# A graph layer with three-digit products: Gelu's result and the last block's sum left in PSUM, and another start

## The chip, the cores and the metric

The kernel runs on one NeuronCore of a Trainium2 chip. The metric is the device time of one execution in microseconds (us). Before the change three runs gave 237.19, 238.38 and 238.70 us; their median is 238.38.

## The reference

One graph layer over 625 nodes of 512 features, 20625 weighted edges and 4 relations. Cut to what is computed:

```
h   = relu(layernorm(x))
msg = sum over r of (h[src] @ W_rel[r] + b_rel[r]) * where(edge_type == r, edge_weight, 0)
agg = segment_sum(msg, dst) / max(segment_sum(edge_weight, dst), 1)
x1  = layernorm(h + h @ W_self + b_self + agg) * ln1_g + ln1_b
ffn = gelu(x1 @ W_ffn1 + b_ffn1) @ W_ffn2 + b_ffn2
out = x + layernorm(x1 + ffn) * ln2_g + ln2_b
```

W_ffn1 is 512 x 1024 and W_ffn2 is 1024 x 512.

## The kernel before

**Tiles.** The nodes lie in five blocks of 125. The engines are TensorE (PE), VectorE (DVE), ScalarE (ACT), GpSimd (POOL) and SyncE (SP, which issues transfers). PSUM is used as eight banks of 128 x 512 words, handed out by `bank(name)`; `row(name)` hands out a row of SBUF.

**Digits.** Most products are not made in f32. An operand is split in a high part, a part between and a low part (fp32r), and three products (high, between, low) replace one f32 product. For Gelu's result g this takes four steps per pair of f: `high_g` (L1135, ACT) rounds g to its high part, `unit_g` (L1138, ACT) scales that up, `between_g` (L1141, DVE) subtracts g, and `low_g` (L1145, DVE) forms the low part. The two DVE steps read g and one other operand.

**Stages.** (1) x is loaded, normalised and turned (`tp_h`, L285; copies `hT`, L671), and multiplied by the weights of the relations into message rows (`pt`, L769; evicted by L777). The first products wait for loads of x (L176, L190, L191), of `firsts` (L194) and of the weights (L188). Ahead of them PE runs warm-up products on `zeros` (L625). (2) DVE decodes the edge lists (L369 to L516; `fields`, L435, go to PE's `tf`, L536) and makes one-hot rows (L557 to L561), which PE adds up (`bank`, L574) and DVE reduces (`sums_w`, L580). (3) Blocks 0 to 2 get their messages by one-hot sums times message rows (`chunk_sum`, L1011). Blocks 3 and 4 get them by 72 indirect transfers that POOL issues (L904), which DVE adds up (L929; the last of them writes `es`), and which PE adds into `acc` (L949, L950, L952). (4) `add_to` (L955) forms the block's sum from `acc`; `block_stats` (L1051), POOL's square root (L280) and `normed` (L1057) make x1; PE turns it (`tp_x`, L285), ACT copies it (`x1T`, L1065). (5) `up` (L1123) makes the first FFN product for one f of eight, into a bank of its own; `act` (L1127) applies Gelu from that bank into a row `gT` in SBUF; the digits follow, and `down` (L1155) makes the second product `po`. (6) `summed` (L1173, L1175), `mean`, the square root, and `normed` (L1187, ACT), `scaled` (L1190, POOL), `added` (L1193, POOL) make the output; POOL also prepares the late copy of x (L1043) and of x1 (L1068, L1071). The last block's end is made in two half columns on DVE (L1197, L1202). Stage 5 is run for blocks 0 and 1 together, 2 and 3 together (250 columns), and 4 alone (125 columns).

**Order.** Every step is handed to the class `Plan` as an `op` with an engine, an estimated duration, its predecessors, a rank, and the buffers that it takes and gives (`ps` are the PSUM banks, `gT` the pairs of f under way). `Plan.times` (L62) goes through time and lets each engine take the best ready op; the code is then emitted in that order, and each engine runs its own instructions strictly in that order. X_AT, W_AT, WARM and `free` are the planner's guesses of when loads arrive. Waits between engines are then set for each tile: an instruction that writes a bank waits for the readers of that bank that were emitted before it, whichever columns they read.

## Time and profile before

| what | before |
| --- | --- |
| median of three runs | 238.38 us |
| the profiled execution's own time | 237.71 us |
| its span | 235.9 us |
| granted TensorE clock | 0.995 |
| PE busy | 220.9 us (94%), 1017 instructions |
| DVE busy | 211.5 us (90%) |
| ACT, POOL busy | 91.5 us, 153.5 us |
| DMA | 43.48 MB, mean 184 GB/s |

The span reaches from the first to the last instruction of the profile; the execution's own time is 1.8 us longer. Rows of the time line give the start in us, the busy time in us, engine, line, operation, output<-inputs, shape, how many instructions the row holds, and in brackets the idle time just before and what ended it. The table of windows gives for each stretch the busy time of each engine. f32 matmuls have two records each.

### The profile page before, as it was taken

What the parts mean: (1) busy time and instruction counts of PE and PEld (TensorE: products, weight loads), DVE (VectorE), ACT (ScalarE), POOL (GpSimd) and SP (SyncE); (2) the same over time, 40 slices, a digit from 0 to 9 for tenths busy, and PEclk for the clock granted to TensorE, in tenths of its full rate; (3) what the DMA queues carried; (4) which work ended last, traced back from release to release, by engine and by line L of the source; (5) the groups of instructions that cost most, each with busy time, mean ns of one, the idle gap of its engine ahead of it and who ended that gap; (6) DMA issues with size and microseconds to landing.
All of it is one profiled execution on the core that took longest, in us unless ns stands there. A gap on an engine that the chain in (4) does not pass through costs nothing. (4 is left out here: it accounts for less than half of the span.)

```text
span 235.9 us, 3270 instructions
## 1 busy us (share of the span) xinstructions
PE 220.9 (94%) x1017; PEld 149.9 (64%) x1017; DVE 211.5 (90%) x404; ACT 91.5 (39%) x181; POOL 153.5 (65%) x167
## 2 busy tenths in 40 slices
PE   6979999999999998999999999999999996999970
PEld 2434445588888786745645444448988884889960
DVE  6996998999999999999999999999999999964542
ACT  2739366494331210103112643225792244635410
POOL 6587830288881067778778778774777899855050
PEclk9999999999999999999999999999999999999997
DMA  6974799868956376789988776678677701100002
GB/s 196 365 236 148 208 259 272 247 164 175 185 136 134 101 257 169 204 332 378 348 280 283 199 208 186 179 213 276 186 199 204 212 6 46 43 0 23 24 3 91
DMA packets 19193, 43.48 MB, mean 184 GB/s; under 512 B 3274, under 2 KB 4180, under 8 KB 19044
## 3 DMA queue, kind: packets, MB, share of 16 engines
q0 software_dynamic: 8272, 22.91, 36.7%
q1 hardware_dynamic: 10498, 19.98, 25.6%
q10 hardware_dynamic: 402, 0.34, 0.5%
q8 instruction: 9, 0.15, 0.3%
q14 instruction: 12, 0.10, 0.1%
HBM read 33.68 MB, written 6.52 MB: 170 GB/s over the span
## 5 line engine op out<-in xcount | busy, mean ns | idle before, releaser
L904 POOL DMA_INDIRECT ms<-table,row_g x72 | 75.7, 1051 | 33.6 <-DVE sums_w L580 12.4
L1011 PE MATMUL acc<-m,sums_w 126*128 126x512 f32 x120 | 53.8, 595 | 0.0
L929 DVE SCALAR_TENSOR_TENSOR ea<-ms,wgt_g,ea 128x512 f32<-128x512 f32 x59 | 41.5, 747 | 0.0
L1011 PEld LDWEIGHTS acc<-m,sums_w 126*128 126x128 f32 x120 | 22.2, 190 | 23.5 <-issue 22.5
L769 PE MATMUL pt<-w,hT 128*128 128x512 f32 x80 | 36.0, 598 | 1.2 <-ACT hT L671 1.2
L1123 PE MATMUL pu<-x1T,w_sb 128*128 128x250 f32 (+1 forms) x192 | 35.7, 341 | 0.0
L1123 PEld LDWEIGHTS pu<-x1T,w_sb 128*128 128x128 f32 x192 | 31.7, 190 | 3.9 <-issue 0.7
L580 DVE TENSOR_REDUCE sums_w<-bank 126x160 f32<-126x480 f32 x48 | 28.0, 651 | 0.0
L769 PEld LDWEIGHTS pt<-w,hT 128*128 128x128 f32 x80 | 14.6, 190 | 17.0 <-issue 13.9
L910 ACT ACTIVATE ea<-ms,groups 128x512 f32<-128x512 f32 x12 | 8.4, 698 | 37.1 <-DMA ms<-table,row_g 36.8
L777 ACT ACTIVATE m<-pt,rx 125x512 f32<-125x512 f32 x20 | 13.7, 685 | 21.9 <-PE pt L769 19.3
L574 PEld LDWEIGHTS <-w_first 128*128 128x128 bf16 x192 | 14.1, 148 | 7.6 <-issue 4.8
L1155 PE MATMUL po<-w_digits,ghigh 128*125 128x512 f32 (+1 forms) x48 | 17.8, 372 | 0.0
L1141 DVE TENSOR_TENSOR gbetween<-glow,gT 128x500 fp32r<-128x500 f32 (+1 forms) x12 | 12.2, 1018 | 6.0 <-ACT glow L1138 6.0
L515 POOL DMA_INDIRECT groups<-in_edge_groups_dram,first_g x12 | 14.5, 1211 | 4.4 <-issue 2.7
L1155 PE MATMUL po<-w_low,glow 128*125 128x512 f32 (+1 forms) x48 | 17.1, 356 | 0.0
L750 POOL DMA_DIRECT2D wd<-w x8 | 8.0, 1188 | 13.7 <-PE pt L769 10.4
L915 ACT CAST eh<-ea 128x512 fp32r<-128x512 f32 x11 | 6.5, 593 | 26.6 <-DVE ea L929 26.5
L574 PE MATMUL bank<-w_first 128*128 128x120 bf16 x192 | 15.5, 227 | 1.3 <-DVE z L780 0.9
L1127 ACT ACTIVATE gT<-pu,cols 128x250 f32<-128x250 f32 (+1 forms) x24 | 10.5, 439 | 13.4 <-PE pu L1123 13.3
L769 PE MATMUL pt<-w_l,hl 128*128 128x512 f32 x40 | 15.7, 392 | 0.0
L769 PE MATMUL pt<-wd,hd 128*128 128x512 f32 x40 | 15.6, 390 | 0.0
(199 smaller groups left out, 415.9 us busy)
## 6 DMA issues: line engine op xcount, KB each, us to landing
table<-m SPq DMA_DIRECT2D x20, 224.0 KB
w<-in_L_gnn_W_rel_dram SPq DMA_DIRECT2D x16, 256.0 KB
wd<-w POOLq DMA_DIRECT2D x8, 256.0 KB, 6.0
w_sb<-in_L_gnn_W_ffn_dram SPq DMA_DIRECT2D x2, 1024.0 KB
w<-in_L_gnn_W_ffn_dram SPq DMA_DIRECT2D x8, 256.0 KB
x_late<-in_x_dram SPq DMA_DIRECT2D x1, 1280.0 KB
ms<-table,row_g POOLq DMA_INDIRECT x72, 3.7
w<-in_L_gnn_W_self_dram SPq DMA_DIRECT2D x4, 256.0 KB
```

Of the source, the lines that this page charges most:

```text
L515: nc.gpsimd.indirect_dma_start(out=groups[:, k].rearrange("p f q -> p (f q)"), out_offset=None, in_=edge_groups[:, :], in_offset=bass.Indi ...
L574: nc.tensor.matmul(p[:, i * W:(i + 1) * W], low[:, t // TB, :, t % TB], high[:, t // TP, :, t % TP], start=True, stop=True)
L580: nc.vector.tensor_reduce(sums_w[OUTER[d]][:NG + 1, :, n0:n0 + 2 * QT].rearrange("p c (t h) -> p t h c", h=2), p[:NG + 1, :QT * 3 * HB].re ...
L769: nc.tensor.matmul(box["p"], x_[:, k, :], w_, start=(k == 0 and n == 0), stop=(k == KD - 1 and n == len(pairs) - 1))
L777: nc.scalar.activation(kept[c][:NG], box["p"][:NG], AF.Copy, scale=rx[:NG, i, root_of(i, r)])
L904: nc.gpsimd.indirect_dma_start(out=ms[j], out_offset=None, in_=table[:, :], in_offset=bass.IndirectOffsetOnAxis(ap=row_g[:, j // EG, j % E ...
L929: nc.vector.scalar_tensor_tensor(to, ms[j], wgt_g[:, k, q - 1:q], box["sum"], op0=ALU.mult, op1=ALU.add)
L1011: nc.tensor.matmul(acc[b,], sums_w[b][:NG + 1, c, :], kept[c][:NG + 1], start=first, stop=last)
L1123: nc.tensor.matmul(p[:, :self.n], w1_sb[0][:, k, f * P:(f + 1) * P], self.x1T()[:, k, :self.n], start=(k == 0), stop=(k == KD - 1))
L1127: nc.scalar.activation(self.gT[f][:, :self.n], self.pu[f][:, :self.n], AF.Gelu, bias=bf1[:, f:f + 1])
L1141: nc.vector.tensor_sub(self.digits(f, "between"), self.low[f, "pair"].bitcast(F32), self.pair[f][:, :, :self.n])
L1155: nc.tensor.matmul(p[:at.stop - at.start, :c.stop - c.start], g_[:, at], w_[:, c], start=(f == 0 and n == 0), stop=(f == KF - 1 and n == l ...
```

## The change

1. **First loads.** The load of x's second block and of `firsts` are issued by ACT in place of SP, so that the four first weight pieces and the rest of x come two places earlier in SP's queue.
2. **Zeros first.** DVE's clearing of `deg_4` and `brel` moves behind the clearing of `zeros`, as an op of the plan; nine warm-up products in place of ten. The planner's guesses (X_AT, W_AT, `free`) are set anew.
3. **Gelu in PSUM.** `up` takes one bank for two f (blocks in pairs) or four f (last block). `act` writes Gelu's result over its own input in that bank. `high_g`, `between_g` and `low_g` read it there. The bank is given back after the last `low_g` on it; `gT` stands at 8 in place of 6.
4. **Last sum in PSUM.** For block 4, `add_to` writes its result into the `acc` bank, and `block_stats` and `normed` read it there; the bank is given back after `normed`.

The diff, cut to its core:

```
-    nc.sync.dma_start(xs[:, 0, :D // 2], x[:P, :D // 2])
-    load_w(0, 0)
-    load_x(xs, 1, 2)
-    nc.sync.dma_start(first_of_tile, firsts)
-    for k in range(1, KD):
+    nc.sync.dma_start(xs[:, 0, :D // 2], x[:P, :D // 2])
+    load_x(xs, 1, 2, nc.scalar)
+    nc.scalar.dma_start(first_of_tile, firsts)
+    for k in range(KD):
         load_w(0, k)
...
-    nc.vector.memset(deg_4, 0.0)
-    nc.vector.memset(brel, 0.0)
+    def cleared():
+        nc.vector.memset(deg_4, 0.0)
+        nc.vector.memset(brel, 0.0)
...
-    WARM = 10
+    WARM = 9
...
-    X_AT = [3.55, 5.4, 9.0, 10.7, 10.7]
-    W_AT = [4.3, 6.7, 7.4, 8.4]
+    X_AT = [3.2, 5.1, 8.0, 9.7, 9.7]
+    W_AT = [4.6, 5.6, 6.4, 7.2]
...
     def add_to(b, of, rows_):
-        nc.vector.scalar_tensor_tensor(z[rows_, b, :], of()[rows_, :], rdeg[rows_, b:b + 1], z[rows_, b, :],
+        sum_of[b] = of() if b == NB - 1 else z[:, b, :]
+        nc.vector.scalar_tensor_tensor(sum_of[b][rows_, :], of()[rows_, :], rdeg[rows_, b:b + 1], z[rows_, b, :],
...
+            self.per = 2 if n > P else 4
...
         def up(self, f):
-            if f % 2 == 0:
-                t = row(f"gT_{self.name}_{f}", F32, (P, 2, 2 * P))
-                self.gT.update({f: t[:, 0], f + 1: t[:, 1]})
-                self.pair[f] = t
-            p = self.pu[f] = bank(f"pu_{self.name}_{f}")
+            m = self.per
+            if f % m == 0:
+                t = bank(f"pu_{self.name}_{f}", (P, m, D // m))
+                self.pu.update({f + q: t[:, q] for q in range(m)})
+                self.pair.update({f + q: t[:, q:q + 2] for q in range(0, m, 2)})
+                if not self.split:
+                    t = row(f"gT_{self.name}_{f}", F32, (P, m, D // m))
+                self.gT.update({f + q: t[:, q] for q in range(m)})
+            p = self.pu[f]
```

The changed code's line numbers are 2 to 12 higher: `up` is L1135, `act` L1139, `high_g` L1147, `down` L1167.

**Place 1: PE in the last block.** `pu_…` is the bank of an `up`, `po_0_2091` and `po_0_2037` are the second product of block 3 (the number counts its column half); "waits Activation" means a wait for ACT. Before:

```order
L1123 MATMUL pu_0_2055<-x1T_2042,w_sb 128x125 [waits Activation_49] x4
L1123 MATMUL pu_1_2064<-x1T_2042,w_sb 128x125 x4
L1123 MATMUL pu_2_2071<-x1T_2042,w_sb 128x125 x4
L1123 MATMUL pu_3_2081<-x1T_2042,w_sb 128x125 x4
L1155 MATMUL po_0_2091<-w_digits_1458,ghigh_0_1928 125x512
```

With the change:

```order
L1167 MATMUL po_0_2037<-w_low,glow_0_1919 125x512
L1135 MATMUL pu_0_2048<-x1T_2031,w_sb 128x125 [waits Activation_49] x4
L1135 MATMUL pu_0_2048<-x1T_2031,w_sb 128x125 x4
L1135 MATMUL pu_0_2048<-x1T_2031,w_sb 128x125 [waits Activation_49]
L1135 MATMUL pu_0_2048<-x1T_2031,w_sb 128x125 x3
L1135 MATMUL pu_0_2048<-x1T_2031,w_sb 128x125 [waits Activation_49]
L1135 MATMUL pu_0_2048<-x1T_2031,w_sb 128x125 x3
L1135 MATMUL pu_4_2077<-x1T_2031,w_sb 128x125 x12
L1135 MATMUL pu_4_2077<-x1T_2031,w_sb 128x125 [waits Activation_49]
L1135 MATMUL pu_4_2077<-x1T_2031,w_sb 128x125 x3
L1167 MATMUL po_0_2037<-w_digits_1460,ghigh_2_1939 125x512
```

Before, the eight `up` stood in two groups of four with twelve products of block 3 between them. Now six products of block 3 stand ahead, all eight `up` follow in one run, and eighteen products of block 3 stand behind. The third, fourth and eighth `up` carry a wait for ACT (the first four rows' wait, for the turned x1, is there in both).

**Place 2: ACT in the last block.** `y_2060` and `y_2044` are block 2's output rows; the store of them stands on ACT's queue. Before:

```order
L1127 ACTIVATE gT_0_2054<-pu_0_2055,cols 128x125 [waits PE_49]
L1127 ACTIVATE gT_0_2054<-pu_1_2064,cols 128x125 [waits PE_49]
L1135 ACTIVATE ghigh_0_2086<-gT_0_2054 128x2x125 [waits Activation_49]
L1138 ACTIVATE glow_0_2089<-ghigh_0_2086 128x2x125 [waits Activation_49]
L1127 ACTIVATE gT_2_2070<-pu_2_2071,cols 128x125 [waits PE_49]
L1187 ACTIVATE y_2060<-y_2060,mv_y_2076 125x512 [waits DMASW1_49,DVE_49,Pool_49]
L1127 ACTIVATE gT_2_2070<-pu_3_2081,cols 128x125 [waits PE_49]
```

With the change:

```order
L1139 ACTIVATE pu_0_2048<-pu_0_2048,cols 128x125 [waits DVE_49,PE_49]
L1199 ACTIVATE y_2044<-y_2044,mv_y_2053 125x512 [waits DVE_49,Pool_49]
L1139 ACTIVATE pu_0_2048<-pu_0_2048,cols 128x125 [waits PE_49,Activation_49]
L1147 ACTIVATE ghigh_0_2074<-pu_0_2048 128x2x125 [waits PE_49,Activation_49]
L1139 ACTIVATE pu_0_2048<-pu_0_2048,cols 128x125 [waits Activation_49]
L1150 ACTIVATE glow_0_2082<-ghigh_0_2074 128x2x125
L1139 ACTIVATE pu_0_2048<-pu_0_2048,cols 128x125 [waits Activation_49]
L1147 ACTIVATE ghigh_2_2092<-pu_0_2048 128x2x125 [waits DVE_49]
L1150 ACTIVATE glow_2_2095<-ghigh_2_2092 128x2x125 [waits DMASW5_49,DMASW0_49,Activation_49]
L1112 DMA out_dram<-y_2044 13x512 [waits Pool_49]
L1139 ACTIVATE pu_4_2077<-pu_4_2077,cols 128x125 [waits PE_49]
L1139 ACTIVATE pu_4_2077<-pu_4_2077,cols 128x125 [waits Activation_49]
```

Gelu now writes the tile that it reads. The normalisation of block 2 moved ahead of the second Gelu, the first `high_g` waits for PE (the fourth `up`), the second `high_g` for DVE (the first `between_g`), and the fifth and sixth Gelu stand behind the store.

**Place 3: SP at the start.** `xs` is x, `w_…` the weight pieces, `w_first` the table `firsts`. Before:

```order
L191 DMA xs<-in_x_dram 128x256
L188 DMA w_0_77<-in_L_gnn_W_rel_dram 128x512
L176 DMA xs<-in_x_dram 128x512
L194 DMA w_first<-in_firsts_dram 128x162
L188 DMA w_1_81<-in_L_gnn_W_rel_dram 128x512
L188 DMA w_2_83<-in_L_gnn_W_rel_dram 128x512
L188 DMA w_3_85<-in_L_gnn_W_rel_dram 128x512
L176 DMA xs<-in_x_dram 128x512 [waits DMAHW0_49]
L176 DMA xs<-in_x_dram 128x2x512 [waits DMAHW1_49]
```

With the change:

```order
L191 DMA xs<-in_x_dram 128x256
L188 DMA w_0_79<-in_L_gnn_W_rel_dram 128x512
L188 DMA w_1_81<-in_L_gnn_W_rel_dram 128x512
L188 DMA w_2_83<-in_L_gnn_W_rel_dram 128x512
L188 DMA w_3_85<-in_L_gnn_W_rel_dram 128x512
L176 DMA xs<-in_x_dram 128x512 [waits DMAHW0_49]
L176 DMA xs<-in_x_dram 128x2x512 [waits DMAHW1_49]
```

Two issues left SP's queue ahead of the second weight piece; both now stand on ACT's queue behind its half of block 0, ahead of the load of the activation table.

More of the change, by code (lines that the diff above doesn't have):

```diff
@@ L173, in gnn_layer, with load_x @@
     first_of_tile = early.take(NT, dtype=I32)
-    def load_x(to, b0, b1):
-        nc.sync.dma_start(to[:, b0:b1, :], bass.AP(tensor=x.tensor, offset=x.offset + b0 * NG * D,
+    def load_x(to, b0, b1, queue=nc.sync):
+        queue.dma_start(to[:, b0:b1, :], bass.AP(tensor=x.tensor, offset=x.offset + b0 * NG * D,
                                                    ap=[[D, P], [NG * D, b1 - b0], [1, D]]))
@@ L604, in gnn_layer @@
     together = [[b, b + 1] for b in range(0, NB - 1, 2)] + [[NB - 1]]
-    plan = Plan(dict(ps=8, add=3, acc=1, one=2, oh=3, low=2, raw=6, row=ROWS - 7, ms=MS, es=6, ow=4, gT=6), free=dict(SP=5.0, Q=10.5), behind=0.6)
+    plan = Plan(dict(ps=8, add=3, acc=1, one=2, oh=3, low=2, raw=6, row=ROWS - 7, ms=MS, es=6, ow=4, gT=8), free=dict(SP=4.2, Q=9.7), behind=0.6)
     op = plan.op
@@ L625, in warm @@
             nc.tensor.matmul(p, zeros[:, :P], zeros, start=True, stop=True)
-    warmed = op("PE", 1.25 + 0.427 * WARM, warm, rank=(0, 0), take=["ps"], give=["ps", "row"])
+    warmed = op("PE", 0.36 * WARM, warm, rank=(0, 0), take=["ps"], give=["ps", "row"], at=1.3)
+    op("DVE", 0.75, cleared, rank=(0, 0), at=2.0)
     turns = []
@@ L952, in edge_sum @@
             nc.tensor.matmul(acc[bs], ohs[0][:, q, :].bitcast(F32), box["sum"], start=first, stop=last)
+    sum_of = {}
     def add_to(b, of, rows_):
-        nc.vector.scalar_tensor_tensor(z[rows_, b, :], of()[rows_, :], rdeg[rows_, b:b + 1], z[rows_, b, :],
+        sum_of[b] = of() if b == NB - 1 else z[:, b, :]
+        nc.vector.scalar_tensor_tensor(sum_of[b][rows_, :], of()[rows_, :], rdeg[rows_, b:b + 1], z[rows_, b, :],
                                        op0=ALU.mult, op1=ALU.add)
@@ L1003, in gnn_layer @@
             m = op("DVE", 0.67, lambda b=b, bs=bs, half_=half_: add_to(b, lambda: acc[bs], half_),
-                   after=[m, own[b]], give=["acc", "ps"] if b == bs[-1] else [], rank=(0.5, n))
+                   after=[m, own[b]], give=["acc", "ps"] if b == bs[-1] != NB - 1 else [], rank=(0.5, n))
             adds[b].append(m)
@@ L1050, in block_stats @@
         st = work.tile([P, 1, 6], F32, tag="bn", name=f"st_z{b}", bufs=4)
-        nc.vector.bn_stats(st[:, 0, :], z[:, b, :])
+        nc.vector.bn_stats(st[:, 0, :], sum_of[b])
         ow["t", b] = aggregate(st, f"z{b}")
@@ L1056, in normed @@
         t = ow["t", b]
-        nc.vector.tensor_scalar(ow["x1", b], z[:, b, :], t[:, 0:1], t[:, 3:4], op0=ALU.subtract, op1=ALU.mult)
+        nc.vector.tensor_scalar(ow["x1", b], sum_of[b], t[:, 0:1], t[:, 3:4], op0=ALU.subtract, op1=ALU.mult)
     def turn_x1(b, box):
@@ L1089, in gnn_layer @@
         s = op("POOL", 0.6, lambda b=b: root(ow["t", b]), after=[s], rank=(-1, b), lag=0.3)
-        s = op("DVE", 0.42, lambda b=b: normed(b), after=[s], take=["row", "ow"], rank=(0.4, b), lag=TURN_LATE)
+        s = op("DVE", 0.42, lambda b=b: normed(b), after=[s], take=["row", "ow"], rank=(0.4, b), lag=TURN_LATE,
+               give=["acc", "ps"] if b == NB - 1 else [])
         t = op("PE", 0.46, lambda b=b, box=box: turn_x1(b, box), after=[s], take=["ps"], rank=(1,), lag=0.4)
@@ L1211, in gnn_layer @@
             d_last = op("PE", 1.72 if two else 0.95, lambda f=f, f_=f_: f_.up(f),
-                        after=[turned[b] for b in blocks] + [d_last, *w1_at], take=["ps"] + (["gT", "row"] if f % 2 == 0 else []),
+                        after=[turned[b] for b in blocks] + [d_last, *w1_at], take=(["ps"] if f % f_.per == 0 else []) + (["gT"] if f % 2 == 0 else []),
                         rank=(4 if two else 3.9, blocks[0], f), lag=0.4)
-            a = op("ACT", 0.46 if two else 0.37, lambda f=f, f_=f_: f_.act(f), after=[d_last, cols_at], give=["ps"],
+            a = op("ACT", 0.46 if two else 0.37, lambda f=f, f_=f_: f_.act(f), after=[d_last, cols_at],
                    rank=(0.9, blocks[0], f))
@@ L1219, in gnn_layer @@
                 a = op("DVE", 0.62 if two else 0.37, lambda f=f, f_=f_: f_.between_g(f - 1), after=[a], take=["row"], rank=(0.46, blocks[0], f))
-                a = op("DVE", 0.62 if two else 0.37, lambda f=f, f_=f_: f_.low_g(f - 1), after=[a], give=["row"], rank=(0.46, blocks[0], f))
+                a = op("DVE", 0.62 if two else 0.37, lambda f=f, f_=f_: f_.low_g(f - 1), after=[a], give=["ps"] if f % f_.per == f_.per - 1 else [], rank=(0.46, blocks[0], f))
                 gel += [a, a]
```

## The prediction

> **What bounds the kernel now.** I read the page first, then PE's waits, then busy time by windows, then the time lines at each place that the change touches.
>
> ```profile
> PE 220.9 (94%) x1017; PEld 149.9 (64%) x1017; DVE 211.5 (90%) x404; ACT 91.5 (39%) x181; POOL 153.5 (65%) x167
> ...
> PE acc L952 <- DVE es L929: 2.3, 1, 2.3
> ...
> PE bank L574 <- DVE z L780: 0.9, 1, 0.9
> ...
> 12.00:18.00 6.00, 4.25 (x19) 2.33 (x18) 5.72 (x18) 2.12 (x5) 5.12 (x8) 1.00 0.72 234
> 18.00:24.00 6.00, 6.00 (x15) 2.66 (x14) 3.96 (x13) 5.94 (x13) 4.72 (x6) 1.00 0.51 146
> 192.00:198.00 6.00, 3.67 (x18) 2.99 (x17) 6.00 (x5) 2.50 (x5) 5.80 (x6) 1.00 0.14 44
> ```
>
> PE is full nearly everywhere (6.00 of 6 in the second window row) and holes are few: the start, 1.75 us between 12 and 18, 0.9 us at a `bank`, 2.33 us around 195, and the tail after 228.4 (rows below). The change removes no product but one warm-up product, so the time moves only by the holes it closes on PE and those it opens. DVE, 90% busy, is the engine that makes two of the holes.
>
> **The hole at 195.** DVE and POOL rows there:
>
> ```profile
> 172.77 0.67 DVE L1141 TENSOR_TENSOR gbetween<-glow,gT 128x500 fp32r<-128x500 f32 x1
> 189.64 0.68 DVE L1173 SCALAR_TENSOR_TENSOR y<-po,z 125x512 f32<-125x512 f32 x1
> 193.43 3.72 DVE L1141 TENSOR_TENSOR gbetween<-glow,gT 128x500 fp32r<-128x500 f32 x1
> 197.06 0.73 DVE L929 SCALAR_TENSOR_TENSOR es<-ms,wgt_g,ea 128x512 f32<-128x512 f32 x1
> ...
> 195.35 1.25 POOL L1043 TENSOR_TENSOR x_late<-x_late,late_rows 128x512 f32<-128x512 f32 x1
> 198.23 1.70 POOL L1043 TENSOR_TENSOR x_late<-x_late,late_rows 128x512 f32<-128x512 f32 x1
> ...
> 204.46 1.00 POOL L280 TENSOR_TENSOR mv_z<-mv_z,half 128x1 f32<-128x1 f32 x1
> ...
> 190.30 5.22 PE L1123 MATMUL pu<-x1T,w_sb 128*128 128x250 f32 x24
> 197.85 1.12 PE L952 MATMUL acc<-es,oh 128*128 128x512 f32 x2 [2.33 <-DVE es L929]
> 206.66 0.60 PE L285 MATMUL tp_x<-ident,x 128*128 128x128 f32 x4
> ```
>
> The same subtraction on two SBUF operands takes 0.67 us when POOL runs none of its elementwise work and 3.72 when it does; L1173, with one operand in PSUM, keeps 0.68 under the same POOL work. With g in PSUM the digit steps become like L1173: `es` comes 3.72 - 0.68 = 3.0 us earlier, near 194.0. PE stood ready at 197.85 - 2.33 = 195.52, with five of eight `up` done; with the change six stand ahead of that product, 1.75 us more (three in 5.22), so PE arrives about 197.3. The wait vanishes: **-2.33 us**. The order alone would nearly do it.
>
> What is late next: the turn of block 4 needs POOL's square root, which ended at 205.46. By the new order PE reaches it after L952 (0.86), two `up` (3.5) and eighteen products of 0.23 us (spacing, below), at about 205.8 less the start's gain; normalisation (0.54) and two hops want the root by some 0.9 us earlier than before. POOL's rows from 198 on are 0.45 us longer than its 1.25; four of them make 1.8 us, which I expect back. Cost 0; if none comes back, about 1.0. For reads or writes in PSUM I take no extra: 0.68 against 0.67 us. In-place Gelu shows in no row; the evictions bound it at about 0.05 us each side.
>
> [...]
>
> **The start.**
>
> ```profile
> 10.00 0.69 DVE L638 BATCH_NORM_STATS2 st_x<-xs 128x6 f32<-128x512 f32 x1
> ...
> 20.14 1.29 DVE L727 TENSOR_TENSOR hd<-hl,hT 128x512 fp32r<-128x512 f32 x2 [1.83 <-ACT hl L723]
> ...
> 32.50 0.56 DVE L435 TENSOR_TENSOR fields<-w_first,fields 128x384 bf16<-128x384 f32 x1
> ...
> 38.90 0.16 DVE L497 COPY ends_g<-groups 128x4 f32<-128x4 f32 x1 [0.25 <-PE groups L494]
> ...
> 41.31 0.86 DVE L475 TENSOR_TENSOR deg_T<-deg_t,deg_T 32x256 fp32r<-32x256 f32 x2 [0.39 <-ACT deg_T L470]
> ...
> 44.81 1.16 DVE L561 TENSOR_TENSOR w_first<-eqs,turned 128x1920 bf16<-128x1920 bf16 x1
> ...
> 15.88 0.62 ACT L676 CAST brel<-brel 128x512 fp32r<-128x512 f32 x1 [4.73 <-DMA brel<-in_brel_dram]
> ...
> 19.45 1.18 ACT L723 ACTIVATE hl<-hh 128x512 fp32r<-128x512 f32 x2
> ...
> 4.13 0.91 SPq L176 DMA_DIRECT2D xs<-in_x_dram  x2
> ...
> 17.04 19.15 PE L769 MATMUL pt<-w,hT 128*128 128x512 f32 x44 [1.16 <-ACT hT L671]
> 36.02 1.00 PE L536 MATMUL tf<-ident_b,fields 128*128 128x128 bf16 x15
> ...
> 46.25 1.15 PE L574 MATMUL bank<-w_first 128*128 128x120 bf16 x16
> ```
>
> Two issues less on SP (0.43 and 0.43 us, half of the 0.91) send the rest of x up to 0.9 us earlier; DVE's statistics of block 2 stood at 10.00. In the new order ACT copies block 2's `hT` ahead of the cast of `brel`, which waited for its load until 15.88 and held up PE until 17.04. So PE can close the 1.75 us of holes in the first window row and start that row of products up to 2.0 us earlier, if the load comes 0.9 earlier; if it lands as late as before, block 2's turn, now ahead of block 1's products, opens a hole of about 1 us and 0.7 remains. But DVE does not gain as much. It waited 1.83 us for ACT's `hl` of blocks 2 and 3; the second of these moves from about 20.6 to 20.3, since ACT's five copies and roundings ahead of it remain. I give DVE 0.4 us there and 0.6 more where it waited for PE (0.25 and 0.39 idle before `ends_g` and `deg_T`). `fields` end at 33.06, three us before PE wants them, but the hots of L561 end at 45.97, 0.28 us before PE takes them at 46.25. So at 46 the gain is PE's, cut to DVE's plus 0.28: 0.7 to 1.3, and I take **-0.9 us**; ends 0 (DVE gains nothing and PE's own slack goes into the 0.9 wait on L780) and -1.9. Clearing `deg_4` and `brel` later costs nothing, since DVE waits for x then; an earlier warm-up lets PE wait longer, not work sooner.
>
> **Banks shared by two f.** An `up` into a bank whose other half already has a Gelu emitted waits for that Gelu. For blocks 0 and 1:
>
> ```profile
> 162.49 0.47 ACT L1127 ACTIVATE gT<-pu,cols 128x250 f32<-128x250 f32 x1 [1.17 <-PE pu L1123]
> 162.99 0.62 ACT L1135 ACTIVATE ghigh<-gT 128x500 fp32r<-128x500 f32 x1
> ...
> 164.18 0.47 ACT L1127 ACTIVATE gT<-pu,cols 128x250 f32<-128x250 f32 x1
> ...
> 166.48 0.68 DVE L1145 SCALAR_TENSOR_TENSOR glow<-gT,glow 128x500 fp32r<-128x500 f32 x1
> ```
>
> The second half of the second bank waits for the third Gelu. Ahead of it on ACT stand two Gelu and two roundings of 0.62, now all behind the second `up` (162.4, 0.1 ahead of the first row): 0.47 + 0.47 + 0.62 + 0.62 + 0.47 ends near 165.3, and PE is ready at 165.1. The other such wait has eight turns on PE as cover; the fourth bank waits for DVE's `low_g`, which ended at 167.2, 4 us before PE gets there. **+0.3 us**, ends 0 and 1.0 (one cast of 0.59 us more ahead on ACT).
>
> **The last block.** One bank holds four f, and ACT, DVE and PE must take turns on it.
>
> ```profile
> 209.65 0.39 PE L1155 MATMUL po<-w_low,glow 128*125 128x512 f32 x1
> 209.88 3.73 PE L1123 MATMUL pu<-x1T,w_sb 128*128 128x125 f32 x32
> 213.37 0.47 PE L1155 MATMUL po<-w_digits,ghigh 128*125 128x512 f32 x1
> ...
> 210.97 0.37 ACT L1127 ACTIVATE gT<-pu,cols 128x125 f32<-128x125 f32 x1 [2.16 <-PE pu L1123]
> ...
> 212.26 0.41 ACT L1135 ACTIVATE ghigh<-gT 128x250 fp32r<-128x250 f32 x1
> ...
> 213.27 0.80 ACT L1187 ACTIVATE y<-y,mv_y 125x512 f32<-125x512 f32 x1
> ...
> 213.15 0.42 DVE L1141 TENSOR_TENSOR gbetween<-glow,gT 128x250 fp32r<-128x250 f32 x1 [1.25 <-ACT glow L1138]
> ...
> 228.42 0.43 DVE L1173 SCALAR_TENSOR_TENSOR y<-po,z 125x256 f32<-125x256 f32 x1 [1.85 <-PE po L1155]
> ```
>
> From the end of block 2's product (T = 209.88 before) PE had 18.5 us of work without a hole. Steps: a product 0.232, an `up` 3.49 / 4 = 0.87, Gelu 0.37 and 0.22 behind its `up`, the normalisation of block 2's output 0.75, a rounding 0.41. With the change: six products to T+1.4, two `up` to 3.1. The first Gelu waits for both and ends at 3.7; the third `up` starts there, 0.6 late, and ends at 4.7. The normalisation of block 2 holds ACT to 4.5, the second Gelu ends at 4.85, the fourth `up` runs 4.9 to 5.8 (0.2 late). Three `up` in the other bank end at 8.4. On ACT: `high` (after the fourth `up`) to 6.4, Gelu, `unit`, Gelu to 7.55; DVE's subtraction 0.42; `high` and `unit` to 8.95, a store's issue (0.36), two Gelu to 10.0. The eighth `up` waits for these: 1.6 late. In all 2.4; I take **+2.3 us** since ACT's rows overlap a little, ends +0.7 (only the last wait, half of it) and +2.9. Nothing else stands on PE to fill it. The digits are ready by T+15.4, before PE wants them.
>
> [...]
>
> The tail after the last product is untouched: block 4's sum in `acc` saves DVE nothing on the path, as its 0.7 us steps stay.
>
> **Sum.** Against the profiled execution's own time, 237.71 (0.67 under the median of 238.38): 237.71 - 2.33 - 0.9 + 0.3 + 2.3 = **237.1 us**.
>
> **Rivals.**
> A, the start's gain is kept whole and the last block's waits are short: -1.9, and 1.0 for both bank terms: 237.71 - 2.33 - 1.9 + 1.0 = 234.5. For it: DVE waits twice for PE and ACT before 46. Against: 0.28 us of slack at the hots, and ACT's queue order in the last block.
> B, slower: the shared banks hand PE's order to ACT in the paired blocks as well, since ACT there also casts for the edges and copies x1T. If each of two waits costs 1.0 and the last block 2.9, and the start is swallowed: 237.71 - 2.33 + 2.0 + 2.9 = 240.3. It decides once these waits exceed 2.33 us. For it: ACT's casts of 0.59; against: ACT is busy 2.50 of 6 us at 192.
> C, the holes only move: PE waits for POOL's root in place of `es` (+1.0) and the start gains nothing, the rest as forecast: 237.71 - 2.33 + 1.0 + 0.3 + 2.3 = 239.0. For it: POOL had no idle time before its root; against: its rows are stretched.
>
> **How the numbers follow.** Forecast 0.44 (own range 236.0 to 238.3), A 0.28, B 0.14, C 0.14. The range takes in A and B to 234.2 and 240.4. Faster by over 1%, which is about what a measurement here can tell from no change, is under 236.0: A and the forecast's low end, 0.35. Slower is over 240.8: a part of B and what I haven't seen, 0.16. The rest, 0.49, is the same.
>
> **What would show it.** No wait of PE on `es`; the digit steps at 0.67 to 0.70 us everywhere; PE's `up` of the last block with three waits on ACT, the longest before the eighth, 18.5 us stretched to about 20.8; the long row of products starting at 15 to 16.3; the hots still just ahead of PE at 45 to 46. A PE with no wait in the last block, or one that waits for L1057 before the turn of block 4, makes the sum wrong.

## The result

The changed kernel takes 238.44 us (median of 17 runs, 237.77 to 241.21) against 237.17 of the kernel before (17 runs): the ratio is 1.0062, with a 95% interval of 1.0037 to 1.0088. A second comparison on another chip (e1 below) gave 238.26 against 237.92, 1.0015 (0.9979 to 1.0051). So the change makes the kernel slower by 0.3 to 1.3 us, of which the second comparison alone could not tell 0.3 from nothing; a gain of 0.6 us was forecast (237.1). On the chips of e1 and e17 about a quarter of the executions of the kernel before took 239 to 240 us at a granted clock of 0.98, which none of e1, e17 and e18 did and of which no trace is kept; without them e1's ratio would be 1.0030. The two profiled executions differ by 0.07 us only (237.78 and 237.71), since that of the kernel before was a long one among its runs and that of the change a short one.

The busy times, the waits of PE (total, times, longest) and the windows of the changed kernel (columns: stretch, PE, PEld, DVE, ACT, POOL, then clock and DMA):

```profile
PE 222.9 (94%) x1016; PEld 150.2 (64%) x1016; DVE 204.8 (87%) x404; ACT 91.3 (39%) x181; POOL 150.6 (64%) x167
```

```profile
PE pu L1135 <- ACT pu L1139: 1.9, 4, 0.8
...
PE bank L576 <- DVE w_first L563: 1.2, 1, 1.2
```

```profile
12.00:18.00 6.00, 6.00 (x21) 2.98 (x20) 5.68 (x19) 3.22 (x7) 5.11 (x8) 1.00 0.68 216
...
102.00:108.00 6.00, 5.30 (x13) 2.22 (x12) 4.35 (x6) 0.59 (x1) 4.78 (x5) 1.00 1.02 393
108.00:114.00 6.00, 5.47 (x27) 3.04 (x27) 5.97 (x10) 1.13 (x2) 4.51 (x5) 1.00 0.72 220
192.00:198.00 6.00, 6.00 (x28) 5.14 (x28) 5.06 (x9) 3.79 (x8) 6.00 (x7) 1.00 0.15 46
210.00:216.00 6.00, 5.08 (x44) 4.71 (x43) 0.42 (x1) 2.68 (x7) 3.03 (x4) 1.00 0.07 20
216.00:222.00 6.00, 5.20 (x31) 4.35 (x30) 2.10 (x5) 3.52 (x10) 0.00 (x0) 1.00 0.09 26
```

The holes of before, at 12 to 18 and at 195, are closed: PE is busy 6.00 of 6 in both. New ones stand where it was full: 102 to 114, and 210 to 222. The kernel before was busy 6.00 of 6 in both windows from 210 to 222, and had at 102 to 114:

```profile
102.00:108.00 6.00, 6.00 (x15) 2.66 (x14) 6.00 (x11) 1.17 (x2) 4.78 (x5) 1.00 1.01 391
108.00:114.00 6.00, 6.00 (x31) 3.64 (x30) 5.93 (x8) 0.69 (x1) 4.79 (x4) 1.00 0.98 355
```

PE's time line of the changed kernel, at the places of the prediction and at the new hole:

```profile
14.91 1.45 PE L772 MATMUL pt<-w,hT 128*128 128x512 f32 x3
...
44.52 1.20 PE L576 MATMUL bank<-w_first 128*128 128x120 bf16 x16
...
108.53 0.67 PE L576 MATMUL bank<-w_first 128*128 128x120 bf16 x8 [1.24 <-DVE w_first L563]
...
197.35 1.02 PE L955 MATMUL acc<-es,oh 128*128 128x512 f32 x2
...
205.76 0.60 PE L284 MATMUL tp_x<-ident,x 128*128 128x128 f32 x4
...
208.95 1.95 PE L1135 MATMUL pu<-x1T,w_sb 128*128 128x125 f32 x16
211.32 1.16 PE L1135 MATMUL pu<-x1T,w_sb 128*128 128x125 f32 x8 [0.43 <-ACT pu L1139]
212.97 3.84 PE L1135 MATMUL pu<-x1T,w_sb 128*128 128x125 f32 x32 [0.49 <-ACT pu L1139]
217.61 1.16 PE L1135 MATMUL pu<-x1T,w_sb 128*128 128x125 f32 x8 [0.80 <-ACT pu L1139]
```

The first `bank` starts 1.73 us earlier than before (46.25; 1.10 in e1's profile). At 108 PE waits 1.24 us. The product on `es` (197.35) and the turn of block 4 (205.76) wait for nothing. The last block has the three waits for ACT. DVE's rows say why PE waits at 108, and that the digit steps are short:

```profile
103.58 2.20 DVE L932 SCALAR_TENSOR_TENSOR ea<-ms,wgt_g,ea 128x512 f32<-128x512 f32 x3 [1.70 <-DMA ms<-table,row_g]
105.69 1.19 DVE L559 TENSOR_TENSOR w_first<-turned,grid 128x2000 bf16<-128x2000 bf16 x1
106.81 0.48 DVE L562 TENSOR_TENSOR eqs<-turned,keys 128x640 bf16<-128x640 bf16 x1
107.32 1.16 DVE L563 TENSOR_TENSOR w_first<-eqs,turned 128x1920 bf16<-128x1920 bf16 x1
...
193.64 0.66 DVE L1153 TENSOR_TENSOR gbetween<-glow,pu 128x500 fp32r<-128x500 f32 x1
...
195.47 0.73 DVE L932 SCALAR_TENSOR_TENSOR es<-ms,wgt_g,ea 128x512 f32<-128x512 f32 x1
```

DVE stood still for 1.70 us until gathered rows (`ms`) had landed. The one-hot step for which PE waits (L559 to L563, ends at 108.48) stood behind three adds of such rows and needs none of them. Where the gain goes shows in three starts of PE's time line (the work of PE ahead of each of the first two is the same in all kernels, but for one warm-up product):

| kernel (profile) | first `bank` | first `up` | last product |
| --- | --- | --- | --- |
| before | 46.25 | 158.92 | 228.10 |
| before, e13 | 46.73 | 159.30 | 227.91 |
| before, e16 | 46.20 | 159.06 | 227.67 |
| changed | 44.52 | 158.25 | 228.30 |
| changed, e1 | 45.15 | 158.72 | 228.86 |
| e4: two f to a bank | 45.03 | 158.39 | 225.90 |
| e17: one-hot step first | 44.86 | 157.22 | 227.07 |
| e14: both | 44.41 | 156.55 | 223.85 |
| e15: two f to a bank, old start | 46.81 | 159.70 | 226.91 |

Two stretches can be read from it. From the first `bank` to the first `up` the kernel before takes 112.6 to 112.9 us and e15, with its start, 112.9; the changed kernel, e1 and e4 take 113.4 to 113.7; e17 and e14 take 112.1 to 112.4. So some 0.8 us of the new start's gain is lost there, and moving one step gives back more than that. From the first `up` to the last product the kernel before takes 69.18, 68.61 and 68.61 us, which is 66.8 to 66.9 in all three once its wait on `es` (below) is taken off. The kernels with four f to a bank in the last block (changed, e1, e17) take 69.9 to 70.1 there, those with two (e4, e14, e15) 67.2 to 67.5.

### The profile page after: what moved, and what is told of

Its sections match the earlier page's. It is cut to its first block, busy times and chain, and to the rows that moved or that the text cites. A ratio compares the mean times of both kernels' runs of the same rounds, so it can differ in the third digit from the quotient of the medians.

```text
span 236.1 us, 3269 instructions
## 1 busy us (share of the span) xinstructions
PE 222.9 (94%) x1016; PEld 150.2 (64%) x1016; DVE 204.8 (87%) x404; ACT 91.3 (39%) x181; POOL 150.6 (64%) x167
## 5 line engine op out<-in xcount | busy, mean ns | idle before, releaser
L1135 PE MATMUL pu<-x1T,w_sb 128*128 128x250 f32 (+1 forms) x192 | 36.5, 343 | 1.9 <-ACT pu L1139 1.9
L1135 PEld LDWEIGHTS pu<-x1T,w_sb 128*128 128x128 f32 x192 | 31.7, 190 | 6.7 <-ACT pu L1139 2.9
L576 PEld LDWEIGHTS <-w_first 128*128 128x128 bf16 x192 | 13.5, 148 | 8.1 <-issue 4.6
L1167 PE MATMUL po<-w_digits,ghigh 128*125 128x512 f32 (+1 forms) x48 | 17.8, 370 | 0.0
L1167 PE MATMUL po<-w_low,glow 128*125 128x512 f32 (+1 forms) x48 | 17.2, 358 | 0.2 <-DVE glow L1157 0.2
L1153 DVE TENSOR_TENSOR gbetween<-glow,pu 128x500 fp32r<-128x500 f32 (+1 forms) x12 | 7.0, 583 | 10.4 <-ACT pu L1139 8.2
L1139 ACT ACTIVATE pu<-pu,cols 128x250 f32<-128x250 f32 (+1 forms) x24 | 9.8, 407 | 16.1 <-PE pu L1135 14.9
```

Source lines behind the costliest of these rows:

```text
L576: nc.tensor.matmul(p[:, i * W:(i + 1) * W], low[:, t // TB, :, t % TB], high[:, t // TP, :, t % TP], start=True, stop=True)
L1135: nc.tensor.matmul(p[:, :self.n], w1_sb[0][:, k, f * P:(f + 1) * P], self.x1T()[:, k, :self.n], start=(k == 0), stop=(k == KD - 1))
L1139: nc.scalar.activation(self.gT[f][:, :self.n], self.pu[f][:, :self.n], AF.Gelu, bias=bf1[:, f:f + 1])
L1167: nc.tensor.matmul(p[:at.stop - at.start, :c.stop - c.start], g_[:, at], w_[:, c], start=(f == 0 and n == 0), stop=(f == KF - 1 and n == l ...
```

## The experiments

The theory (L in the expectations): the forecast terms stand, but the start's gain, which the prediction followed as far as 46, is lost at 108, where DVE's order holds a one-hot step behind gathered rows. Medians in us, and ratios to the kernel before on the same chip (ratios of means, so they are not quite the quotients of the medians):

| run | what | time | before | ratio (95%) |
| --- | --- | --- | --- | --- |
| e1 | changed kernel again | 238.26 | 237.92 | 1.0015 (0.9979 to 1.0051) |
| e2 | parts 1 and 2 alone | 245.96 | 237.92 | 1.0328 (1.0265 to 1.0391) |
| e3 | parts 3 and 4 alone | 238.89 | 237.92 | 1.0022 (0.9990 to 1.0055) |
| e4 | change, two f to a bank | 235.69 | 237.92 | 0.9892 (0.9833 to 0.9951) |
| e14 | e4, one-hot step first | 233.80 | 237.24 | 0.9876 (0.9851 to 0.9900) |
| e15 | e4, old start | 236.87 | 237.24 | 0.9979 (0.9952 to 1.0006) |
| e17 | change, one-hot step first | 236.85 | 238.53 | 0.9940 (0.9904 to 0.9976) |
| e18 | change without part 4 | 238.35 | 238.53 | 1.0014 (0.9984 to 1.0043) |

**e1, the changed kernel again.** No edit.

> The changed kernel once more, for a second profile beside the first, which fell on the low end of its own runs. Theory L (the start's gain is lost again between 103 and 109, where DVE stands with hots queued behind adds that wait for gathered rows; the hole at 195 and the last block's waits cancel): PE's gain over the kernel before is about 1.7 us at the first `bank`, at most 0.7 at the first `up` (158) and 0 at the last product, with one idle stretch of DVE of 1.5 us or more on gathered rows near 104. Rival V (the loss lies elsewhere and varies from run to run): a profile of a typical run shows holes of PE of 1 us or more at other places than the first profile. Time: 1.003 to 1.009 of the kernel before.

Its profile has the same holes as the first: 1.1 us on `w_first` at 109, 1.9 on ACT in the last block, none on `es`; DVE waits 1.6 us for gathered rows. So the second theory, V, falls for these two profiles: the lost time is not at places that come and go. L's sizes were partly missed: PE's gain was 1.10 us at the first `bank` (1.7 expected) and 0.20 at the first `up`, the last product came 0.76 later than in the profile of before, and the ratio lay under the expected 1.003 to 1.009.

**e2, the start alone.** The kernel before with

```
-    load_w(0, 0)
-    load_x(xs, 1, 2)
-    nc.sync.dma_start(first_of_tile, firsts)
-    for k in range(1, KD):
+    load_x(xs, 1, 2, nc.scalar)
+    nc.scalar.dma_start(first_of_tile, firsts)
+    for k in range(KD):
...
-    WARM = 10
+    WARM = 9
...
+    op("DVE", 0.75, cleared, rank=(0, 0), at=2.0)
```

and the planner's new guesses.

> Parts 1 and 2 of the change alone (loads, zeros, warm-up and the planner's guesses); Gelu and the last sum as before. The order of all engines up to the first `up` is that of the changed kernel. Theory L: the row of products starts 2.1 us earlier, the first `bank` 1.7, but at the first `up` 0.7 or less is left, and the hole at `es` takes that: 0.997 to 1.002 of the kernel before. Rival D (the start pays in full and the digits in PSUM lose it): 0.993 or less. Rival S (the new order of gathers and hots itself costs time): 1.003 or more.

It took 8.0 us more. That is S by the number, but not by its cause; L's number (0.997 to 1.002) is missed, since it took the hole on `es` to stay as it was. PE's order up to the first `up` is that of the change, and that `up` starts at 158.06, 0.86 earlier than in the profile of before; then one wait takes that and much more. PE, DVE and POOL of e2:

```profile
204.99 1.22 PE L953 MATMUL acc<-es,oh 128*128 128x512 f32 x1 [7.83 <-DVE es L930]
```

```profile
195.65 8.63 DVE L1146 SCALAR_TENSOR_TENSOR glow<-gT,glow 128x500 fp32r<-128x500 f32 x1
```

```profile
195.16 1.26 POOL L1194 TENSOR_TENSOR y<-y,x_late 125x512 f32<-125x512 f32 x1
196.39 1.25 POOL L1191 TENSOR_TENSOR y<-y,late_rows 125x512 f32<-125x512 f32 x1
197.62 2.47 POOL L1044 TENSOR_TENSOR x_late<-x_late,late_rows 128x512 f32<-128x512 f32 x2
200.05 1.25 POOL L1194 TENSOR_TENSOR y<-y,x_late 125x512 f32<-125x512 f32 x1
201.27 2.47 POOL L1044 TENSOR_TENSOR x_late<-x_late,late_rows 128x512 f32<-128x512 f32 x2
209.07 0.91 POOL L279 TENSOR_TENSOR mv_z<-mv_z,half 128x1 f32<-128x1 f32 x1 [5.33 <-DVE mv_z L274]
```

A digit step of 0.67 us with both operands in SBUF was held for 8.63 us: POOL ran seven elementwise instructions without a pause from 195.16 to 203.74 at their usual 1.25 us each, and the step ended at 204.28, 0.54 after the last of them. In e2 six `up` stand ahead of the product on `es`, as in the changed kernel, where POOL runs just as full (6.00 of 6 from 192 to 198) and that product waits for nothing. So it is g in PSUM that closes the hole, and not the order.

The wait is not the whole loss. PE had been idle since 197.16, and on the page of e2 (40 slices of 6.1 us, a digit each: PE's busy share and its granted clock in tenths of full speed, 9 for 0.9 or more) the clock has a 9 in every slice up to 200.8 us, 5 in the slice from there to 206.9 and 8 in the next, to 213.0:

```profile
PE   7999999999999999989999999999999943999970
...
PEclk9999999999999999999999999999999995899996
```

The first of the two records of the product on `es` took 1.22 us there (204.99, above), against 0.70 in the kernel before and 0.59 in the changed kernel.

**e3, Gelu and last sum in PSUM alone.** The changed kernel with the lines of e2 turned back.

> Parts 3 and 4 alone (Gelu's result and the last sum in PSUM) with the start of the kernel before. The order of all engines up to the first `up` is that of the kernel before. Theory L: no wait on `es`, digit steps of DVE at 0.7 us, three waits in the last block that sum to about 2.2; net 0 to +0.5 us, 1.000 to 1.002 of the kernel before. Rival D: 1.005 to 1.009, as slow as the whole change. Rival S: 0.999 or less.

PE's waits in e3:

```profile
PE pu L1134 <- ACT pu L1138: 2.2, 4, 1.1
```

No wait on `es`; four for ACT instead. The time lies 0.97 us over the median of before, between L (up to 0.5) and D (1.2 to 2.1); the ratio, 1.0022, is L's within its interval. So the time alone does not part the two. Against e1, on the same chip, the new start saves 238.89 - 238.26 = 0.63 us: it does not pay in full, as D needs.

**e4, two f to a bank everywhere.**

```
-            self.per = 2 if n > P else 4
+            self.per = 2
```

> The whole change, with two f to a bank in the last block too (`per` = 2 everywhere). By the theory that the last block's waits come from four f sharing a bank, the long wait before the eighth `up` goes, at most one short wait is left, and the time falls by 1.5 to 2.2 us against the changed kernel: 0.996 to 1.000 of the kernel before. Rival: ACT's Gelu and casts set the pace there anyway, the waits move to `down` behind the digits, and the time falls by less than 0.5 us: 1.004 or more.

The waits of PE for ACT shrink from 1.9 to 0.2 us in all, that at 108 stays:

```profile
PE bank L576 <- DVE w_first L563: 1.0, 2, 0.9
...
PE pu L1135 <- ACT pu L1139: 0.2, 1, 0.2
```

The time falls by 238.26 - 235.69 = 2.57 us, somewhat more than expected. So four f in one bank are what the last block's waits come from, and nothing behind them takes their place.

**e13 and e16, the kernel before again.** No edit.

> The kernel before, for a second profile on a chip where it takes 236 to 239 us. Theory P (the held-up DVE step ends only when POOL's run of elementwise work pauses, so its length is not the same in each execution): the step is not 3.72 us and the wait of PE on `es` not 2.33, but anything from 0.5 to 4, and the time moves with the wait. Rival: the same step of 3.6 to 3.8 us and the same wait of 2.2 to 2.4, and the time moves for other reasons.

> The kernel before, for a third profile. Theory P: again another length of the held-up step and of the wait on `es`; over the profiles the time follows the wait. Rival: the same wait of 2.2 to 2.4 us in all.

First the rows of e13, then of e16:

```profile
197.65 0.70 PE L952 MATMUL acc<-es,oh 128*128 128x512 f32 x1 [1.75 <-DVE es L929]
```

```profile
193.21 3.73 DVE L1141 TENSOR_TENSOR gbetween<-glow,gT 128x500 fp32r<-128x500 f32 x1
```

```profile
197.44 1.12 PE L952 MATMUL acc<-es,oh 128*128 128x512 f32 x2 [1.77 <-DVE es L929]
```

```profile
193.00 3.72 DVE L1141 TENSOR_TENSOR gbetween<-glow,gT 128x500 fp32r<-128x500 f32 x1
```

Theory P is wrong as it was put, for these three profiles: the step takes 3.72 or 3.73 us each time, and each time it ends 0.54 or 0.55 us after the start of POOL's first pause (0.2 us long), which comes at the same point of POOL's order. But the wait is not always 2.33: PE came to it at 195.52, 195.90 and 195.67, and `es` let it go at 197.85, 197.65 and 197.44. The wait is the distance between two engines that drift by some tenths. The profile of the prediction was the one with PE early and DVE late; the other two, of 237.43 and 237.15 us, lie nearer to the usual time.

**e17, the changed kernel with the one-hot step first.**

```
         order = self.times()
+        hots = [i for i, o in enumerate(order) if o.engine == "DVE" and o.us == 2.7][-3]
+        adds = [i for i in range(hots) if order[i].engine == "DVE" and order[i].us == 0.67 and order[i].rank[0] == 2]
+        order.insert(adds[-3], order.pop(hots))
```

> The changed kernel as it is (four f to a bank in the last block), with the one-hot step ahead of the three adds of gathered rows and nothing else. Theory L: PE's wait of 1.2 us near 108 goes, with the 0.4 behind it at 114, and stays gone to the end, while the last block's waits stand at 2.2 to 2.5 us: 1.5 to 2.0 us under the changed kernel, 0.994 to 0.998 of the kernel before. Rival M (a hole opens later instead, or the last block's waits grow by what was won): within 0.6 us of the changed kernel, 1.000 or more.

PE's waits in e17:

```profile
PE pu L1138 <- ACT pu L1142: 1.9, 4, 0.8
...
PE bank L579 <- DVE w_first L566: 0.4, 2, 0.2
```

236.85 us against 238.35 of e18 on the same chip (which is the changed kernel but for part 4, and that makes no difference, below): 1.5 us, as L had it. The first `up` comes at 157.22, 1.0 to 1.5 us earlier than in the two profiles of the change, and the last product at 227.07, 1.2 to 1.8 earlier. The last block's waits are the same 1.9 us, so they do not swallow the gain: M falls. The place of this one step of DVE is what loses the start.

**e14, both edits.** e4 with the lines of e17.

> The same kernel as e5 and e9 (two f to a bank everywhere, one one-hot step ahead of three adds of gathered rows). Theory L: PE's wait of 0.9 to 1.2 us on `w_first` near 108 goes and stays gone: 0.7 to 1.1 us under two f to a bank alone (0.989 in e4), a ratio of 0.984 to 0.987. Rival M (the hole only moves to a later wait for the delayed adds): 0.988 or more.

DVE's time line of e14 at the place, and all waits of PE that its list has from 0.2 us:

```profile
99.72 2.06 DVE L935 SCALAR_TENSOR_TENSOR ea<-ms,wgt_g,ea 128x512 f32<-128x512 f32 x3
101.70 1.19 DVE L562 TENSOR_TENSOR w_first<-turned,grid 128x2000 bf16<-128x2000 bf16 x1
...
104.40 2.07 DVE L935 SCALAR_TENSOR_TENSOR ea<-ms,wgt_g,ea 128x512 f32<-128x512 f32 x3
```

```profile
PE warm L630 <- DVE zeros L203: 1.3, 1, 1.3
PE pu L1138 <- ACT pu L1142: 0.2, 1, 0.2
PE pt L775 <- DVE sums_w L585: 0.2, 1, 0.2
```

The step now runs while the rows are on their way, and the adds behind it find them landed. 233.80 us, faster than either kernel: 0.9876 of before. That lies between L's range (0.984 to 0.987) and M's (0.988 or more), and e4 ran on another chip, so the ratio does not decide. The profiles do: from the first `bank` to the first `up` e14 takes 112.14 us against 113.36 in e4, and what is won is not lost behind it (67.30 against 67.51 to the last product).

**e15, two f to a bank with the old start.** e4 with the lines of e2 turned back.

> The same kernel as e6 and e10 (two f to a bank everywhere, the start of the kernel before). Theory L: hole at 195 closed, pairs +0.5, last block nothing: 0.991 to 0.995 of the kernel before, 0.4 to 1.3 us over two f to a bank with the new start. Rival V (the last block's waits swallowed the start's gain in the whole change): 0.996 or more.

0.9979: a gain of 0.4 us where L gave 1.2 to 2.1, so the number is V's. With the usual hole of 1.76 in place of 2.33 and 0.5 for the pairs, L gives 1.3; PE's last product, at 226.91, lies 0.8 to 1.2 before those of the kernel before. V's reason is refuted by e17, where the last block's waits stand and the gain arrives. Behind the first `up` the profile has all that L gave: 67.21 us to the last product, as e4 and e14, against 68.6 to 69.2 of the kernel before. What it lacks lies outside that stretch: of the profiles of the table it has the latest first `bank` (46.81) and the longest end (its span of 235.0 us reaches 8.1 past the start of the last product, those of the kernel before 7.6 to 7.8). Whether that is so in every execution is open, and the ratio's interval is 0.6 us to either side.

**e18, the last sum in SBUF.**

```
-        sum_of[b] = of() if b == NB - 1 else z[:, b, :]
+        sum_of[b] = z[:, b, :]
```

and the bank given back by `add_to`.

> The whole change without the last sum in PSUM, on another chip than e7 and e11. Prediction: within 0.3 us of the changed kernel, 1.000 to 1.008 of the kernel before, with steps of 0.7 to 0.8 us for the sum and 0.5 to 0.8 for the normalisation. Rival: these steps of DVE, now on SBUF operands, are held up by POOL's elementwise work, and the turn of block 4 comes 0.5 us or more later: 1.008 or more.

1.0014, as e1 has 1.0015: part 4 neither costs nor saves what these runs can tell. PE's waits in e18 are those of the changed kernel (1.9 us for ACT, 1.1 on `w_first`), with none at the turn of block 4, so the rival (1.008 or more) falls.

**e5 to e12.** These ran on two other chips, where every kernel took longer and PE stood at a lower granted clock in some stretches (5 tenths on the pages from 125.8 to 132.4 us and from 205.2 to 211.8 in e12, from 195.2 to 201.7 in e10). The same kernels as e14 (e5, e9: 251.39 and 253.75 us), e15 (e6, e10: 267.93 and 266.38), e18 (e7, e11: 254.75 and 255.32), the kernel before (e12: 266.59; 267.93 and 265.33 were its medians) and e8. The waits in question can't be told there from others (of 4.1 us in e5, 5.6 in e12 and 8.1 in e8). With the old start a kernel took about 30 us more than on the other chips, with the new one 16 to 20; why, is open. So there the change, without its part 4, took 0.9589 (e7; 0.9453 to 0.9725) and 0.9643 (e11; 0.9584 to 0.9701) of the kernel before, a gain that no theory here gave: that it makes the kernel slower holds for the other chips only. None of these runs tells L from its rivals, and the kernels were run again as e13 to e18.

> The changed kernel with two f to a bank everywhere (as in the run before), and one more edit: the second one-hot step of the last dense block stands ahead of the three adds of gathered rows that DVE waited 1.3 to 1.7 us for near 104, instead of behind them; nothing else moves. Theory L (this wait is what loses the start's gain at 108): DVE's idle time on gathered rows goes or shrinks under 0.4, PE's wait of 0.9 to 1.2 us on `w_first` at 108 goes, and the time falls by 0.7 to 1.1 us against the run with two f to a bank (235.7): about 234.8, 0.985 to 0.988 of the kernel before. Rival M (the hole only moves: the adds are late instead, and PE waits for `el`, or for the next gathered rows, before 120): less than 0.3 us of it is left at the last product, 235.4 or more.

> Two f to a bank everywhere, with the start of the kernel before (its loads, zeros, ten warm-up products, guesses). Theory L: against the kernel before, the hole at 195 closes (-2.3 us) and the pairs cost 0.5, the last block nothing: about 1.8 us faster, 0.992 to 0.995; and against two f to a bank with the new start the old start costs 0.4 to 0.9 us, the same small gain that the whole change got from it. Rival V (the start's gain is eaten only because the last block's waits for ACT swallow it): the old start costs 1.5 us or more, so the time is within 0.4 us of the kernel before.

> The whole change without its part 4: block 4's sum goes to SBUF as before, Gelu stays in PSUM; the order of every engine is that of the changed kernel. By the prediction the last sum in PSUM costs and saves nothing: within 0.3 us of the changed kernel, 1.000 to 1.006 of the kernel before, with `add_to`, the statistics and the normalisation of block 4 at 0.7 to 0.8 and 0.5 us. Rival: these steps of DVE on two SBUF operands are held up by POOL as the digit steps were (POOL has elementwise work from 195 to 203), and the root, the turn of block 4 and the last product come 0.5 us or more later.

> The same kernel as e5 (two f to a bank everywhere, one one-hot step ahead of three adds of gathered rows), on a chip where the gathered rows come in time. Theory L: PE's wait of 0.9 to 1.2 us on `w_first` near 108 goes and stays gone: 234.5 to 235.1 us if the kernel before takes 237.5, a ratio of 0.987 to 0.990. Rival M (the hole only moves to a later wait for the delayed adds): 0.991 or more, as two f to a bank alone or slower.

> The same kernel as e6 (two f to a bank everywhere, the start of the kernel before). Theory L: hole at 195 closed (-2.3 us), pairs +0.5, last block nothing: 0.991 to 0.995 of the kernel before. Against two f to a bank with the new start (0.989 in e4) the old start then costs 0.4 to 1.3 us. Rival V (the last block's waits swallowed the start's gain in the whole change): the old start costs 1.7 us or more, 0.996 or more of the kernel before.

> The same kernel as e7 (the whole change without the last sum in PSUM). Prediction: 0.3 us or less from the changed kernel, so 1.000 to 1.008 of the kernel before, with steps of 0.7 to 0.8 us for the sum and 0.5 to 0.6 for the normalisation. Rival: DVE's sum, statistics or normalisation of block 4 are held up by POOL's elementwise work and the turn of block 4 comes 0.5 us or more later: 1.008 or more.

> The kernel before, for a second profile. The profile that the prediction is built on had one DVE step of 3.72 us and a wait of PE on `es` of 2.3. Theory P (the step ends when POOL's run of elementwise work pauses, and how long that takes is not the same in each execution): the step and the wait have another length here, the wait between 0.5 and 4 us, and the time moves with it. Rival: the same step of 3.6 to 3.8 us and the same wait of 2.2 to 2.4.

Only e8 says something by its rows. It is e2 with

```
-lambda b=b: nc.gpsimd.tensor_add(x_late["x"][:, b, :], x_late["x"][:, b, :], b2_bc())
+lambda b=b: nc.gpsimd.tensor_add(x_late["x"][:, b, :8], x_late["x"][:, b, :8], b2_bc()[:, :8])
```

> Parts 1 and 2 alone again, with POOL's additions to the late copy of x cut from 512 to 8 columns (the output lacks the second bias of the FFN in the other columns); the order on all engines is as with parts 1 and 2 alone. There one digit step of DVE with both operands in SBUF took 8.63 us, from 195.65 until POOL's unbroken run of elementwise work ended at 203.74. Theory P (POOL's run keeps such a step of DVE out until POOL pauses): the step ends within 0.6 us of the first pause of POOL, the wait of PE on `es` falls from 7.8 us to under 2, and the time falls by 6 us or more, to 0.995 to 1.010 of the kernel before. Rival (the step is slow for another reason, transfers or a late operand): it stays over 6 us and the time over 1.025.

DVE and POOL of e8:

```profile
213.81 1.47 DVE L1142 TENSOR_TENSOR gbetween<-glow,gT 128x500 fp32r<-128x500 f32 x1
...
215.86 1.10 DVE L1146 SCALAR_TENSOR_TENSOR glow<-gT,glow 128x500 fp32r<-128x500 f32 x1
```

```profile
213.48 1.26 POOL L1194 TENSOR_TENSOR y<-y,x_late 125x512 f32<-125x512 f32 x1
214.70 1.72 POOL L1191 TENSOR_TENSOR y<-y,late_rows 125x512 f32<-125x512 f32 x1
```

With less POOL work, the step that took 8.63 us takes 1.10, the one ahead of it 1.47, and PE's wait on `es` is gone from its list. Here the two engines took turns: DVE's first step ended at 215.28, 0.54 after POOL's first instruction, and POOL's second took 0.46 longer than usual. So POOL's work has its part in holding the step, as P says. But P's own sign, an end at POOL's first pause, did not come: POOL ran without a pause until 219.17 and the step ended at 216.96. The time itself says nothing on that chip. Why DVE got its turn after one instruction here and not for seven in e2, no run settles.

## Why the prediction was wrong, point by point

| term | forecast | measured |
| --- | --- | --- |
| hole at 195 | -2.33 | gone in e1, e3, e4, e14, e15, e17 and e18; 1.75 and 1.77 in two more profiles of before |
| start | -0.9 | -0.63 (e1 against e3); in the two profiles 1.1 and 1.7 at the first `bank`, 0.2 and 0.7 at the first `up` |
| pairs | +0.3 | +0.4 to +0.7 (first `up` to last product in e15, e14 and e4, less 66.85) |
| last block | +2.3 | +2.57 (e4 against e1); 2.55 in the profile |
| sum | -0.6 | about +0.7 |

The sum of what was measured, -1.76 - 0.63 + 0.5 + 2.57 = +0.7 us, lies between the two comparisons (+0.3 and +1.3). Every wait that the prediction named came, or went, as it said; four sizes were off, all to the same side. It did not have the wait at 108 (nor a short one of 0.19 us at 181). So the step that failed in kind is the -0.9 us for the start, which was followed no further than 46; the others are sizes: the hole at 195 for the gain, and the two terms of shared banks.

**The hole at 195: right in kind, the size taken from one execution.** It closes because the digit step takes 0.66 us in place of 3.72, as argued from L1173. "The wait vanishes: -2.33 us" is the largest miss in the gain: the profiled execution lay 0.54 us over the median of its 17 runs, and 0.57 of the wait was not there in the other two profiles. For the time forecast, 237.1, it costs nothing, since the sum starts from that same execution: 237.71 - 2.33 and 237.17 - 1.76 both give 235.4. Of the 1.3 us by which 238.44 lies over 237.1, 0.7 comes from the other three terms, 0.2 to 0.3 each by the table; the other 0.6 is not in the profiled execution of the change (237.78) and stays open. The order alone would not "nearly do it": e2 has six `up` ahead of that product and a wait of 7.8 us.

**The start: the step that failed in its reasoning.** The prediction cut PE's gain to DVE's at 46 and took -0.9. There nothing was cut: PE kept 1.73 us in the profile (1.10 in e1's). But it ended its search at 46. The next place where PE has to wait for DVE is 108. The gathered rows come in POOL's stream of transfers, which had won 0.50 us (its first starts at 83.28, before at 83.78); three adds of such rows stood ahead of a one-hot step, DVE waited 1.70 us for them, and PE 1.24. At the first `up` 0.67 of the gain was left. e17 moves that one step and has 1.5 us back. Rival C ("the holes only move") was nearest in time, with 239.0, and had the right fate for the start; its mechanism, a wait for POOL's root, did not come: the root of block 4 took 0.54 us as expected, and no product waited for it.

**Banks shared by two f: right, slightly low.** The wait at the second half of the second bank is there, 0.23 us idle at 164.4; a second one for DVE's `glow`, 0.19 at 181.4, was not foreseen.

**The last block: right, a little low.** Three waits came, on the third, fourth and eighth `up`, the longest before the eighth, and 18.5 us became 228.58 - 207.56 = 21.0 (20.8 expected), with 228.58 the end of the last product and 207.56 the end of block 2's (208.95 less six products). The split was off: at 0.87 us for an `up` the third started 0.62 late, the fourth 0.78 and the eighth 1.15, in place of 0.6, 0.2 and 1.6. (The idle times in the brackets, 0.43, 0.49 and 0.80, are shorter, since the row ahead of each runs on for longer than that spacing: 1.95 us for the first two `up`, in place of 1.74.) ACT's rows show it:

```profile
211.20 0.80 ACT L1199 ACTIVATE y<-y,mv_y 125x512 f32<-125x512 f32 x1
212.58 0.34 ACT L1139 ACTIVATE pu<-pu,cols 128x125 f32<-128x125 f32 x1 [0.58 <-PE pu L1135]
...
216.84 0.71 ACT L1139 ACTIVATE pu<-pu,cols 128x125 f32<-128x125 f32 x2
```

The normalisation of block 2 ended before the third `up` did, so the second Gelu did not wait for it but for PE; ACT's 0.58 idle there became PE's wait before the fourth. The last two Gelu ended at 217.55, and PE went on at 217.61.

**PSUM operands: right for the digit steps, wrong for one other.** 0.66 and 0.68 us for a digit step from PSUM (193.64 and 197.00 in the changed kernel), 0.67 from SBUF undisturbed (172.77 in the kernel before). But the normalisation of block 4, which part 4 lets read PSUM, takes longer than the same step of the other blocks in the changed kernel (mean ns behind the busy time):

```profile
L1063 DVE TENSOR_SCALAR x<-z,mv_z 128x512 f32<-128x512 f32 x4 | 2.2, 566 | 0.5 <-POOL mv_z L279 0.5
...
L1063 DVE TENSOR_SCALAR x<-acc,mv_z 128x512 f32<-128x512 f32 x1 | 0.8, 810 | 2.0 <-POOL mv_z L279 2.0
```

In the kernel before, from SBUF, block 4's takes 0.54 us (205.68). So "I take no extra" missed 0.27 us there; it costs nothing, as the turn of block 4 waits for nothing. Part 4 as a whole: nothing, as said (e18).

**B, slower by shared banks in the pairs,** did not happen: the two waits there have 0.23 and 0.19 us of idle time.

## What to carry to other kernels

When one engine gets ahead, look through the rest of the order for every place where the other engine was just in time, and ask which of its waits do not move with it: here, transfers in a stream of their own. Work that needs no transfer belongs ahead of work that waits for one (1.5 us in e17). A hole between two engines is the difference of two arrival times, and one profile of it is one sample: take it from two or three before it becomes a term of a sum. A buffer shared by four writers and a reader in turn costs what the turns cost (2.57 us here); with two to a bank the same edit became a gain (e4: 0.9892 of before). A long wait can cost more than its own length: look at the granted clock behind it (5 tenths in e2, in and behind a wait of 7.8 us).
